# Layer 2's edge scores: the two channel halves' edge products set apart, their score products put together, ten edge buffers

## The chip, the cores and the metric

The kernel runs on one core of one Trainium2 chip. The metric is device time in microseconds (us) of one execution, as the median of several runs. A core has five engines that work side by side: TensorE (PE, matrix products; PEld is its weight load), VectorE (DVE), ScalarE (ACT), GpSimd (POOL) and SyncE (SP, which here only issues transfers). Each takes its own list of instructions in order, and semaphores make one engine wait for another.

## The reference

Four graph layers run one after another, each wrapped as `x = layernorm(x + layer(x, adj))`. The tensor x is 128 graphs x 64 nodes x 256 channels, all in f32. Only layer 2 is touched by the change:

```
Xq = (H @ W_lin.T).reshape(bt, n, 4, 64)          # 4 heads of 64 channels
Xv = (H @ W_val.T).reshape(bt, n, 4, 64)
e  = einsum('behd,hd->beh', leaky_relu(Xq[:, src] + Xq[:, dst], 0.2), a)   # 512 edges
e  = e + log(adj[src, dst] + 1e-8)
attn = softmax of e over the edges that share a src
Y  = segment_sum(attn * Xv[:, dst], src);  return Y @ W_out.T
```

For every graph and each of its 512 edges the rows of Xq at the edge's two ends are added, passed through a leaky relu, and multiplied with a vector per head: these sums are the scores.

## The kernel before, in words

X, the running tensor, stays on the chip as 64 tiles of 128 rows (two graphs of 64 nodes) x 256 channels. The scores of layer 2 are made by the generator `scores()`, in 32 steps k of two tiles each, that is four graphs (b = 0, 1 within a tile, i = 0, 1 for the tile). A step consists of the following.

- `transposed(k)`: four full transposes of X on PE (L1988) into a PSUM tile m; DVE copies it to xT (L1990).
- `maps(k)`: eight PE instructions of 128 x 128 x 512 (L2000; an f32 product is two instructions in the profile) make Xq and Xv in two PSUM tiles m; ACT copies them out as xq (L2004) and xv (L2014), and SP stores xv to DRAM (L2015) for later. The pool of m tiles has two buffers.
- For each channel half c = 0, 1 the edge products (L2037): four f32 products `xq.T @ GG` (GG holds a one at both ends of each edge), one for each (b, i), in the order (0,0), (1,0), (0,1), (1,1). Each uses 64 of the array's 128 rows: b = 0 the upper half, b = 1 the lower half. They write two PSUM tiles l (one for each i, with room for b = 0 and 1).
- ACT copies every l half to an edge buffer xs of 128 x 512 (L2044), and DVE applies the leaky relu in place (L2045). There are six xs buffers.
- `products()`: the score products (L1976), four f32 products of 128 rows x 32 columns, which add xs times the head vectors to the PSUM tile sc of this half c. They are called one half late: the products of the half before are issued behind the edge products of this half.

Beside this, the generator `last_pass()` finishes layer 1, four steps of it for each k: ACT scales Y (L1893), PE transposes it into an m tile (L1902), DVE adds it to X and gathers statistics (L1234, L1237, L1238), and once in each k a `Norm.flush()` takes a square root on ACT (L1214), five small DVE instructions (L1215 to L1249) and four normalisations of 128 x 256 on ACT (L1253). It lasts until k = 14. From k = 15 on the softmax of the first half of the graphs (`softmax(0)`, from L2059) is woven in, and from k = 26 on `values()`: products of 64 x 64 (L2143) and the output product (L2164).

The source order is a priority and not the order of execution: the framework's scheduler fixes the order of each engine's instructions when the program is built, and may place a later instruction ahead of one whose inputs are not due yet. `after(ins, those)` adds dependencies by hand: before the change the first of a half's four edge products waits for all earlier copies out of l and m (`taken`), so that the four stand together, and the first score product is ordered behind the last edge product and waits for all leaky relus of its half.

Of the kernel before, what the change touches and what calls it, by code (L numbers as in the profile page):

```python
# [7 lines left out]
F32 = mybir.dt.float32  # L8
I32 = mybir.dt.int32
AF = mybir.ActivationFunctionType  # L10
ALU = mybir.AluOpType
# [3 lines left out]
N = 64  # L15
NB = 128
D = 256
P = 128
E = 512
# [1240 lines left out]
def tile_adj_resnorm(ctx: ExitStack, tc: tile.TileContext, I: dict, out: bass.AP, layers: int = 4):  # L1260
    nc = tc.nc
    v, s, te = nc.vector, nc.scalar, nc.tensor
# [10 lines left out]
    for b in range(2):  # L1273
        r, o = slice(b * N, (b + 1) * N), slice((1 - b) * N, (2 - b) * N)
# [235 lines left out]
    with tc.tile_pool(name="lw", bufs=1) as lw, tc.tile_pool(  # L1510
        name="l0c", bufs=1
    ) as lc, tc.tile_pool(name="l0p", bufs=2, space=PSUM) as pp, tc.tile_pool(
        name="l0r", bufs=1, space=PSUM
# [196 lines left out]
        with tc.tile_pool(name="l0g", bufs=1) as l0:  # L1710
            back = iter(())
            for g in range(NT // TG):
# [7 lines left out]
                last, more = H, iter(())  # L1720
# [203 lines left out]
    HU = HT // 2  # L1924
    with ExitStack() as l2:
# [4 lines left out]
        sx = own1(scoring, name="l2x", bufs=2, side="right")  # L1930
        pg = own1(scoring, name="l2g", bufs=2, space=PSUM)
        pc = own1(scoring, name="l2c", bufs=2, space=PSUM)
        edge_s = lt.tile([P, WE], F32, tag="edge_s", name="edge_s")
        nc.sync.dma_start(edge_s, edge_d)
        GG, OS, lg, br, OE, ix = edge_tables(edge_s)
# [10 lines left out]
        az = lt.tile([P, 2, 3 * HU - 1], F32, tag="az", name="az")  # L1946
# [3 lines left out]
                o = (h + 1) * HU - 1  # L1950
                v.tensor_tensor(az[:, c, o : o + 1], heads[:, h : h + 1], acol[:, c : c + 1], ALU.mult)
        bf, bb = br[:, :E], br[:, 1:]
        sc, M2 = [None, None], [None, None]

        xvd = [dl.tile([P, 2, D], F32, tag=f"xv{k}", name=f"xv{k}") for k in range(NT // 2)]

        taken, late = [], []
        beside = [iter(())]
        soft = []

        def after(ins, those, how=mybir.DependencyClass.Sync):
            for i in those:
                tc.add_manual_dep(ins.ins, i.ins.name, mybir.DependencyInfo(how, mybir.DependencyReason.DATA),
                                  reason="together")

        def products():

            k, c, xs, ready = late.pop()
            half, u_ = divmod(k, HU)
            if u_ == 0 and c == 0:  # L1970
                sc[half] = [pc.tile([P, 512], F32, tag="sc", name="sc") for _ in range(2)]
            mms = []
            for b in range(2):
                for i in range(2):
                    q = 32 * (2 * b + i)
                    mms.append(te.matmul(sc[half][c][q : q + 32, :], az[:, c, HU - 1 - u_ : 3 * HU - 1 - u_],  # L1976
                                         xs[b, i], start=(u_ == 0), stop=(u_ == HU - 1)))
            after(mms[0], ready)
            if u_ == HU - 1:
                run(*[soft[half]] * (2 if half and not c else 1))  # L1980
            return mms[0]

        def transposed(k):

            ps = pp.tile([P, 512], F32, tag="m", name="m")
            for i in range(2):
                for c in range(2):
                    te.transpose(ps[:, i * D + c * P : i * D + (c + 1) * P], X[:, 2 * k + i, c * P : (c + 1) * P], ident)  # L1988
            xT = sx.tile([P, 2, 2, P], F32, tag="xT", name="xT", bufs=1)
            v.tensor_copy(xT.rearrange("p i c n -> p (i c n)"), ps)  # L1990
            return xT

        def maps(k, xT, apart=False):

            xq, xv = [], sx.tile([P, 2, D], F32, tag="xv", name="xv")
            pss = [pp.tile([P, 512], F32, tag="m", name="m") for _ in range(2)]

            def product(i, cols):
                for c in range(2):
                    te.matmul(pss[i][:, cols], xT[:, i, c, :], wqv[:, c, cols], start=(c == 0), stop=(c == 1))  # L2000

            def first(i):
                xq.append(sx.tile([P, D], F32, tag="xq", name="xq", bufs=4))
                taken.append(s.copy(xq[i], pss[i][:, :D]))  # L2004

            if apart:
                for i in range(2):
                    product(i, slice(0, D))
                    first(i)
            for i in range(2):  # L2010
                product(i, slice(D, 2 * D) if apart else slice(0, 2 * D))
                if not apart:
                    first(i)
                s.copy(xv[:, i, :], pss[i][:, D:])  # L2014
            nc.sync.dma_start(xvd[k], xv)  # L2015
            return xq

        def scores():


            K = NT // 2
            xT = transposed(0)
            xq = maps(0, xT, True)
            next(beside[0])
            next(beside[0])
            xT = transposed(1)


            four = [(b, i) for i in range(2) for b in range(2)]
            for k in range(K):  # L2030
                xn = None
                for c in range(2):
                    xs, pl = {}, [pg.tile([P, 2, 512], F32, tag="l", name="l") for _ in range(2)]
                    mms = []
                    for b, i in four:
                        r = slice(b * N, (b + 1) * N)
                        mms.append(te.matmul(pl[i][:, b, :], xq[i][r, c * P : (c + 1) * P], GG[r, :], start=True, stop=True))  # L2037
                    after(mms[0], taken)
                    del taken[:]
                    next(beside[0], None)  # L2040
                    ready = []
                    for b, i in four:
                        x = xs[b, i] = sx.tile([P, E], F32, tag="xs", name="xs", bufs=6)
                        taken.append(s.copy(x, pl[i][:, b, :]))  # L2044
                        ready.append(v.scalar_tensor_tensor(x, x, 0.2, x, ALU.mult, ALU.max))  # L2045
                    if late:
                        after(products(), mms[-1:], mybir.DependencyClass.NoSync)
                    late.append((k, c, xs, ready))
                    if c == 0 and k < K - 1:
                        xn = maps(k + 1, xT)  # L2050
                    if c == 1 and k < K - 2:
                        xT = transposed(k + 2)
                    next(beside[0], None)
                xq = xn
                if k == K - 1:
                    products()
                yield

        def softmax(half):  # L2059
# [108 lines left out]
        def run(*steps):  # L2168
            for x in steps:
                next(x, None)  # L2170

        bank = None
        scratch = lambda: bank() if bank else pp.tile([P, 512], F32, tag="m", name="m")
        sc_, beside[0] = scores(), last_pass()
        run(*beside * 4)
        run(*[sc_] * (NQ - 1))
# [40 lines left out]
        with tc.tile_pool(name="l3s", bufs=2) as s3, tc.tile_pool(name="l3p", bufs=6, space=PSUM) as p3:  # L2217
# [3 lines left out]
            four = lambda a: a.rearrange("p (j n) -> p j n", j=4)  # L2221
# [121 lines left out]
```

## Time and profile before

| | us |
|---|---|
| median of three runs | 2368.93 (2366.29 to 2371.05) |
| the profiled execution | 2368.87 |
| its span on the core | 2367.1 |
| edge products (L2037) first and last start | 1786.2 and 2156.9 |
| PE busy in the span | 2282.1 (96%) |
| DVE busy | 1804.4 (76%) |
| ACT busy | 971.7 (41%) |
| PE busy on L2037, 512 instructions | 134.0 |
| PE busy on L1976, 512 instructions | 68.2 |
| ACT busy on L2044, 256 instructions of 585 ns | 136.6 |
| DVE busy on L2045, 256 instructions of 683 ns | 165.9 |

Every stretch of time is read from the start of the span. In the timeline a row stands for a run of like instructions: start, length from the first start to the last end, engine, line, operation, output <- inputs, shape, count, and in brackets the idle time of the engine before it with what ended it. As PE instructions overlap at their ends, the step from one row's start to the next row's start is what a group takes.

### The profile page before, as it was taken

The page shows a single profiled execution, that of the slowest core. Times are in us where ns is not written, and L with a number is a line of the kernel's source. Part 1 is how long each engine was busy: PE and PEld are TensorE (multiplying, and loading weights), DVE is VectorE, ACT ScalarE, POOL GpSimd, SP SyncE. Part 2 cuts the span into 40 slices and gives each one's busy share as a digit, 9 for nine tenths or more (in the row PEclk, how much of TensorE's full clock was granted, in tenths as well). Part 3 has the DMA queues.
Part 4 walks back from the last instruction along what each step waited for, and adds up shares of the span by engine and source line. Part 5 has one row for each costly group of instructions (what it writes and reads, how often), then busy time and mean ns, then how long its engine had stood idle before and what let it go on. Part 6 is the DMA issues. An engine that isn't in the chain of part 4 may idle for free. (4 is left out here: it accounts for less than half of the span.)

```text
span 2367.1 us, 29693 instructions
## 1 busy us (share of the span) xinstructions
PE 2282.1 (96%) x9094; PEld 1228.0 (52%) x9094; DVE 1804.4 (76%) x8366; ACT 971.7 (41%) x1754; POOL 88.0 (4%) x134
## 2 busy tenths in 40 slices
PE   8999999999999999999999999999999999999897
PEld 6445654444665544664544544454434333445787
DVE  5666666677987888888889897787867886646587
ACT  2432232242333243332243322343437875557575
POOL 0000000000000000000000000000000000101431
PEclk9999999999999999999999999999999999999999
DMA  6000010100100010100101010011210010311532
GB/s 222 23 16 36 1 36 1 36 19 18 54 1 36 1 54 19 54 25 12 36 18 44 28 36 1 1 70 74 86 55 23 27 40 27 103 36 43 138 93 72
DMA packets 44662, 101.52 MB, mean 43 GB/s; under 512 B 5297, under 2 KB 23857, under 8 KB 43217
## 3 DMA queue, kind: packets, MB, share of 16 engines
q1 hardware_dynamic: 38656, 84.90, 10.6%
q0 software_dynamic: 3984, 14.40, 2.2%
q8 instruction: 72, 1.18, 0.2%
q14 instruction: 94, 0.76, 0.1%
q10 hardware_dynamic: 1856, 0.28, 0.1%
HBM read 67.97 MB, written 31.59 MB: 42 GB/s over the span
## 5 line engine op out<-in xcount | busy, mean ns | idle before, releaser
L1621 PE MATMUL pq<-H,wi 128*128 128x512 f32 (+1 forms) x2016 | 828.3, 547 | 4.6 <-DVE H L1671 4.0
L1648 ACT ACTIVATE gate<-pq,bl 128x512 f32<-128x512 f32 (+1 forms) x504 | 316.5, 633 | 761.6 <-PE pq L1626 618.7
L1621 PEld LDWEIGHTS pq<-H,wi 128*128 128x128 f32 x2016 | 372.3, 190 | 332.6 <-issue 255.8
L1626 PE MATMUL pq<-lh,wh 128*128 128x512 f32 (+1 forms) x1152 | 471.3, 533 | 12.0 <-DVE lh L1666 11.1
L1626 PEld LDWEIGHTS pq<-lh,wh 128*128 128x128 f32 x1152 | 215.1, 190 | 210.9 <-issue 135.0
L2045 DVE SCALAR_TENSOR_TENSOR xs<-xs 128x512 f32<-128x512 f32 x256 | 165.9, 683 | 57.0 <-ACT xs L2044 56.0
L2044 ACT COPY xs<-l 128x512 f32<-128x512 f32 x256 | 136.6, 585 | 73.8 <-PE l L2037 40.5
L1664 ACT ACTIVATE gate<-lc 128x512 f32<-128x512 f32 (+1 forms) x144 | 83.6, 580 | 183.0 <-DVE lc L1660 85.3
L2037 PE MATMUL l<-edge_s,xq 64*128 64x512 f32 x512 | 134.0, 616 | 9.5 <-ACT xs L2044 4.8
L2000 PE MATMUL m<-wqv,xT 128*128 128x512 f32 (+1 forms) x264 | 121.0, 595 | 0.9 <-DVE xT L1990 0.8
L1811 PE MATMUL ps<-at,w 128*128 128x512 f32 x256 | 116.7, 607 | 4.0 <-ACT at L1807 3.5
L1861 PE MATMUL ps<-h,w 128*128 128x512 f32 x256 | 112.3, 596 | 2.4 <-ACT h L1855 2.4
L1253 ACT ACTIVATE X<-X,ln_sh,ln_rs 128x256 f32<-128x256 f32 x192 | 99.9, 591 | 31.1 <-DVE ln_sh L1249 22.9
L142 DVE COPY AQR<-eps 64x192 f32<-64x192 f32 (+1 forms) x125 | 35.1, 281 | 94.3 <-PE eps L148 94.3
L1237 DVE BATCH_NORM_STATS2 ln_st<-X 128x6 f32<-128x256 f32 x256 | 98.6, 416 | 2.4
L2000 PEld LDWEIGHTS m<-wqv,xT 128*128 128x128 f32 x264 | 46.7, 189 | 73.9 <-issue 55.0
L1861 PEld LDWEIGHTS ps<-h,w 128*128 128x128 f32 x256 | 47.9, 190 | 60.7 <-issue 50.7
L1811 PEld LDWEIGHTS ps<-at,w 128*128 128x128 f32 x256 | 47.1, 192 | 59.9 <-issue 46.9
L2037 PEld LDWEIGHTS l<-edge_s,xq 64*128 64x128 f32 x512 | 46.1, 186 | 60.6 <-issue 31.7
L1671 DVE TENSOR_TENSOR H<-gate 128x512 f32<-128x512 f32 (+1 forms) x72 | 46.7, 649 | 30.5 <-ACT gate L1664 27.0
L129 DVE SCALAR_TENSOR_TENSOR CS<-GA,qE 64x1 f32<-64x1 f32 x294 | 61.7, 210 | 9.6
L1976 PE MATMUL sc<-xs,az 128*32 128x512 f32 x512 | 68.2, 605 | 0.6 <-DVE xs L2045 0.5
(585 smaller groups left out, 3200.5 us busy)
## 6 DMA issues: line engine op xcount, KB each, us to landing
wi<-in_WihT_dram SPq DMA_DIRECT2D x16, 1024.0 KB, 4.9
wh<-in_WhhT_dram SPq DMA_DIRECT2D x12, 1024.0 KB, 6.7
xd<-X SPq DMA_DIRECT2D x16, 512.0 KB, 3.0
X<-xd SPq DMA_DIRECT2D x16, 512.0 KB, 3.4
xv<-xv SPq DMA_DIRECT2D x32, 256.0 KB, 2.0
xr<-xv POOLq DMA_DIRECT2D x32, 256.0 KB, 3.0
X<-in_x_dram SPq DMA_DIRECT2D x15, 512.0 KB, 8.9
out_dram<-X SPq DMA_DIRECT2D x15, 512.0 KB, 2.9
```

What stands on the lines that cost most here:

```text
L1237: nc.vector.bn_stats(st, self.X[:, k, :])
L1253: nc.scalar.activation(x, x, AF.Identity, bias=sh[:, k : k + 1], scale=rs[:, k : k + 1])
L1621: te.matmul(ps, wi[:, kk, o * P : (o + 1) * P], at(kk, k), start=(kk == 0), stop=(k == 0 and kk == 1))
L1626: te.matmul(ahead[gt, c], wh[:, kk, o * P : (o + 1) * P], hst[:, kk, :M], start=False, stop=(kk == 1))
L1648: s.activation(gates[gt][:, c, :M], ps, AF.Tanh if gt == 2 else AF.Sigmoid, bias=bl[:, p - 1, o : o + 1])
L1664: s.activation(g[2], cs, AF.Tanh)
L1811: te.matmul(ps, w1[:, k, c * P : (c + 1) * P], at[:, k, :], start=(k == 0), stop=(k == 1))
L1861: te.matmul(ys[c], w2[:, k, c * P : (c + 1) * P], h[:, k, :], start=(k == 2), stop=(k == 1))
L2000: te.matmul(pss[i][:, cols], xT[:, i, c, :], wqv[:, c, cols], start=(c == 0), stop=(c == 1))
L2037: mms.append(te.matmul(pl[i][:, b, :], xq[i][r, c * P : (c + 1) * P], GG[r, :], start=True, stop=True))
L2044: taken.append(s.copy(x, pl[i][:, b, :]))
L2045: ready.append(v.scalar_tensor_tensor(x, x, 0.2, x, ALU.mult, ALU.max))
```

## The change

In step k the edge products of half 0 come first, then `last_pass` (two steps), the maps of step k + 1, `last_pass` again (two steps), the transposes for step k + 2, the edge products of half 1, and then, in one call, the score products of half 1 of step k - 1 and of half 0 of step k: eight in a row. The last step adds the products of its half 1. The edge buffers go from six to ten. The waits are by tile: the first product into the l tile of i waits for the copies out of the l tile of the same i one half earlier (`taken[i]`), and in half 0 for the copy of xq[i] (`mapped[i]`); the four edge products of a half no longer wait together. The first of the eight score products waits for the leaky relus of both its halves and is ordered behind the last edge product. The sc tiles are allocated one by one.

```diff
-        sc, M2 = [None, None], [None, None]
+        sc, M2 = [[None, None], [None, None]], [None, None]
...
-        taken, late = [], []
+        taken, mapped = {}, {}
...
-        def products():
-            k, c, xs, ready = late.pop()
...
+        def products(todo, held, last):
+            xss = [held.pop(x) for x in todo]
             mms = []
+            for (k, c), (xs, _) in zip(todo, xss):
+                half, u_ = divmod(k, HU)
+                if u_ == 0:
+                    sc[half][c] = pc.tile([P, 512], F32, tag="sc", name="sc")
+                for b in range(2):
+                    for i in range(2):
+                        q = 32 * (2 * b + i)
+                        mms.append(te.matmul(sc[half][c][q : q + 32, :], az[:, c, HU - 1 - u_ : 3 * HU - 1 - u_],
+                                             xs[b, i], start=(u_ == 0), stop=(u_ == HU - 1)))
+                if u_ == HU - 1:
+                    run(*[soft[half]] * (2 if half and not c else 1))
+            after(mms[0], [x for _, ready in xss for x in ready])
+            after(mms[0], [last], mybir.DependencyClass.NoSync)
...
-                taken.append(s.copy(xq[i], pss[i][:, :D]))
+                mapped[i] = s.copy(xq[i], pss[i][:, :D])
...
+            held = {}
+            def edges(c):
+                xs, ready = {}, []
+                for i in range(2):
+                    pl = pg.tile([P, 2, 512], F32, tag="l", name="l")
+                    for b in range(2):
+                        r = slice(b * N, (b + 1) * N)
+                        mm = te.matmul(pl[:, b, :], xq[i][r, c * P : (c + 1) * P], GG[r, :], start=True, stop=True)
+                        if not b:
+                            after(mm, taken.pop(i, []) + ([mapped[i]] if c == 0 else []))
+                    for b in range(2):
+                        x = xs[b, i] = sx.tile([P, E], F32, tag="xs", name="xs", bufs=10)
+                        taken.setdefault(i, []).append(s.copy(x, pl[:, b, :]))
+                        ready.append(v.scalar_tensor_tensor(x, x, 0.2, x, ALU.mult, ALU.max))
+                held[k, c] = xs, ready
+                return mm
             for k in range(K):
-                xn = None
-                for c in range(2):
...
+                edges(0)
+                xn = None
+                run(*beside * 2)
+                if k < K - 1:
+                    xn = maps(k + 1, xT)
+                run(*beside * 2)
+                if k < K - 2:
+                    xT = transposed(k + 2)
+                last = edges(1)
                 xq = xn
+                todo = [(k - 1, 1)] * (k > 0) + [(k, 0)]
+                products(todo, held, last)
                 if k == K - 1:
-                    products()
+                    products([(k, 1)], held, last)
                 yield
```

More of the change, by code (lines that the diff above doesn't have):

```diff
@@ L1964, in after @@
                                   reason="together")
-        def products():
-            k, c, xs, ready = late.pop()
-            half, u_ = divmod(k, HU)
-            if u_ == 0 and c == 0:
-                sc[half] = [pc.tile([P, 512], F32, tag="sc", name="sc") for _ in range(2)]
-            mms = []
[L1973 to L1981, printed above, removed]
+        def products(todo, held, last):
+            xss = [held.pop(x) for x in todo]
+            mms = []
+            for (k, c), (xs, _) in zip(todo, xss):
[11 more added lines that the diff above has]
+            after(mms[0], [last], mybir.DependencyClass.NoSync)
         def transposed(k):
@@ L2026, in scores @@
             xT = transposed(1)
-            four = [(b, i) for i in range(2) for b in range(2)]
+            held = {}
[14 more added lines that the diff above has]
+                return mm
@@ L2030, in scores @@
             for k in range(K):
+                edges(0)
                 xn = None
-                for c in range(2):
[L2033 to L2053, printed above, removed]
```

## The prediction

> **What bounds the kernel now.** I read the page's busy shares, then the windows, then the timeline of one score step, since all that changes lies between 1786 and 2162 us.
>
> ```profile
> PE 2282.1 (96%) x9094; PEld 1228.0 (52%) x9094; DVE 1804.4 (76%) x8366; ACT 971.7 (41%) x1754; POOL 88.0 (4%) x134
> ```
> ```profile
> 1900.00:1950.00 50.00, 48.82 (x230) 19.52 (x229) 42.93 (x113) 39.23 (x87) 0.00 (x0) 1.00 0.12 37
> ...
> 2000.00:2050.00 50.00, 49.78 (x238) 20.54 (x237) 29.88 (x47) 26.26 (x57) 8.94 (x9) 1.00 0.11 35
> ```
> PE, the first number after the length, is full in both stages. Beside the last pass DVE has 42.93 of 50 and ACT 39.23; later both have room. One step beside the last pass (PE and two rows of ACT):
> ```profile
> 1862.67 1.99 PE L2037 MATMUL l<-edge_s,xq 64*128 64x512 f32 x8
> ...
> 1864.59 1.07 PE L1976 MATMUL sc<-xs,az 128*32 128x512 f32 x8
> ...
> 1865.59 0.66 PE L1988 MATMUL m<-ident,X 128*128 128x128 f32 x4
> ...
> 1866.08 0.60 PE L1902 MATMUL m<-ident,y 128*128 128x128 f32 x4
> ...
> 1866.71 2.08 ACT L1253 ACTIVATE X<-X,ln_sh,ln_rs 128x256 f32<-128x256 f32 x4
> 1866.80 0.30 PEld L2037 LDWEIGHTS l<-edge_s,xq 64*128 64x128 f32 x4 [0.36 <-ACT xs L2044]
> 1866.80 1.99 PE L2037 MATMUL l<-edge_s,xq 64*128 64x512 f32 x8
> ...
> 1868.69 1.04 ACT L2044 COPY xs<-l 128x512 f32<-128x512 f32 x2
> ...
> 1868.72 1.07 PE L1976 MATMUL sc<-xs,az 128*32 128x512 f32 x8
> ...
> 1869.71 3.70 PE L2000 MATMUL m<-wqv,xT 128*128 128x512 f32 x8
> ...
> 1873.25 0.60 PE L1902 MATMUL m<-ident,y 128*128 128x128 f32 x4
> ```
> The next step's edge products start at 1873.88: 11.20 us a step (half 0 from 1866.80, half 1 at 1873.88). From start to start: a half's edge products 1.92, its score products 0.99, maps 3.54, transposes then edge products 0.62. The edge rows work in pairs, one for each half of the rows: 8 instructions take four slots of 0.43. ACT shows one more thing: the copy at 1868.69 could have started 1.18 after its products (2006.43 to 2007.61 elsewhere), at 1867.98, but stood behind four normalisations. PE had other work meanwhile.
>
> The price of a lone edge product is in the later stage:
> ```profile
> 2089.78 1.12 PE L2037 MATMUL l<-edge_s,xq 64*128 64x512 f32 x2 [0.24 <-ACT xs L2044]
> ...
> 2090.83 1.99 PE L2164 MATMUL m<-wo,yT 128*128 128x256 f32 x8
> ...
> 2092.76 1.98 PE L2037 MATMUL l<-edge_s,xq 64*128 64x512 f32 x6
> ...
> 2093.92 1.07 ACT L2044 COPY xs<-l 128x512 f32<-128x512 f32 x2 [2.68 <-PE l L2037]
> ...
> 2094.67 1.07 PE L1976 MATMUL sc<-xs,az 128*32 128x512 f32 x8
> ```
> One product alone takes 1.05, and the other three still 1.91, as much as all four. The copy of the first l tile waits for both its products, so it starts only 1.16 after the second.
>
> **The change part by part.** It removes and adds no arithmetic; it moves instructions. I read the new order from the built program, with what each instruction waits for. In steps 2 to 14 PE runs:
>
> ```
> edge 0 (i=0: 2 products), L1902 x3, edge 0 (i=1: 2), L1902 x1, maps 8,
> L1902 x4, edge 1 (1 product), L1988 x4, edge 1 (3 products), score products (16)
> ```
> The scheduler has split both halves, since the four no longer wait together. ACT runs: copy l1/i0, square root, copy l1/i0, four normalisations, two copies l1/i1, four copies of edge 0, then Y, xq, xv.
>
> *First stage, PE alone.* sc 1.91 (four slots 1.71 and a change to the row products, 0.2), edge pair 1.06, L1902 x3 0.51, pair 1.06, L1902 0.2, maps 3.54, L1902 0.62, lone 1.05, L1988 0.62, three 1.91: 12.48, so 1.28 above 11.20. The step from score products straight to edge products occurs nowhere in the trace; its bounds are 0 and 0.21 (edge to score, 1.92 less four slots); nearest is score to full, 0.14. I take 0.2. It costs nothing here, as the wait below covers it.
>
> *First stage, the new wait.* The second pair of edge 0 needs the l tile of i = 1, so it needs the two copies l1/i1, which ACT holds behind the normalisations. With t = 0 at L1988: three edge products from 0.62; first copy 0.62 + 1.18 = 1.80; the square root after it at 2.3 (its input, after L1990 at 0.63 to 1.31 and the statistics, is there at 1.7); leaky relu 2.41 (copy + 0.61), reciprocal 3.05, second relu 3.25 (0.64), four small DVE steps (1854.50 to 1855.31: 0.2 each) bring the shift at 4.50, normalisations at 4.69 (+0.19), the next copy 1.99 later (1855.50 to 1857.49) at 6.68, both done at 7.74, PE goes on at 7.80. PE alone would be there at 6.0: it waits 1.8. From there: pair 1.06, L1902 0.2, maps 3.54, L1902 0.62, lone 1.05, and L1988 again at about 14.24. The step grows by 3.04. Twelve of them (L1988 of step 1 to that of step 13): **+36.5**. Entry: L1988 of step 1 falls at about 1807.5 (1786.23 and the same rows, with about 1.4 of waits), so step 2 starts at 1811.9 against 1810.79: +1.1. Step 14 runs 12.6 against 13.07, and 0.6 of waits in the steps before goes: -1.0.
>
> *Ten edge buffers.* The two copies l1/i1 need buffers that the first score products free, at score start + 1.08 (2008.35 to 2009.43) = 3.6, before 6.68: nothing here. Later they run from 9.1 to 10.2 of a step and edge 0's second pair is due at 10.8: hidden by 0.6; without that cover it costs up to 0.5 a step.
>
> *Later stage, steps 15 to 25* (1958.84 to 2076.63, 117.8). Mostly the halves stay whole: edge 1.92, maps 3.54, L1988 0.62, edge 1.92, score 1.91: 9.91 against 10.19 (1996.24 to 2006.43), as four changes of tile shape stand where six were. Eleven times -0.28 is -3.1; step 16 has a lone product (+1.2); and before had already run four map instructions when step 15 began, 1.9, while after must still run them. Waits of 3.2 (softmax) I keep: about **0** (+0.5 taken).
>
> *Steps 26 to 30* (2076.63 to 2148.41, 71.8). Before, a lone edge product is split off in each; after, only in step 26, and L2143 and L2164 stand behind the score products. A step: 9.91 + 0.90 (L2143) + 1.92 (L2164) less 0.06 = 12.7, and about 0.35 in which L2164 waits for ACT's copy yT. Three such, step 26 with two L2143 groups 15.1, step 30 without L1988 12.4: 66.6, **-5.2**.
>
> *Step 31* (2148.41 to 2161.83, 13.4). Both edge halves stand together; the second waits for copies until 2.3 and 3.4 after the start, score products at 4.4, the last four at 7.5, end at 8.5: -4.9. But one L2164 and six L2143, 2.2, move behind the end: **-2.7**. The transfers keep their number and their place behind their copies: SP's xv stores follow the xv copies as before, POOL's loads follow L2143.
>
> *Sum* on the profiled execution, 2368.87 (median of the runs 2368.93, no difference): +1.1 + 36.5 - 1.0 + 0.5 - 5.2 - 2.7 = +29.2, 2398.1 us.
>
> The Trainium skill, TensorEngine Tiling (Array Packing), section Key Properties, says that a change of tiling mode drains the array; TensorE: Matmul & The Clock Gate, Step-by-step, gives a drain of about 128 cycles. The rows above show more, 0.14 to 0.21 a change. By an estimate from that page (128 cycles at 2.4 GHz, 0.05) the -3.1 of steps 15 to 25 would be about -1.2, and the sum 2400.
>
> **The rivals.**
>
> *B: the copies come in time.* If the second pair's wait doesn't show, the step is PE's own 12.48: 12 x 1.76 and as much in step 14 less, 22.9: 2375. For it: in the row at 1868.69 the same copies stood behind the same block at no cost. Against: there the next edge pair was 5 us away.
>
> *C: the later stage gives nothing back*, because copies, yT and the normalisations of `values` queue on one ACT as in 2139.55 to 2144.28, where PE already waited. Without the -5.2 and -2.7: 2406.
>
> *D, the other side: faster.* The first stage is held by DVE and not by PE's order: 42.93 of 50 is 9.6 us in 11.20, and DVE's work is unchanged. If the step stays at 11.20 whatever PE's order, the +36.6 falls away: 2361.5. It decides where a step grows by less than 7.4 / 12 = 0.6, below 11.8 us. Against it: PE has 48.82 of 50, and the lone product alone adds 1.05.
>
> **How the numbers follow.** My sum 0.64, B 0.14, C 0.17, D 0.05. A measurement tells about 0.2%, 4.7 us, from no change. The range 2377 to 2409 holds my own case (2388 to 2406 by itself: a step of 13.6 to 14.6) and C with three more for longer waits; it leaves out D and most of B. B at 2375 is itself just beyond the bound for slower, so a part of it counts as the same: slower 0.91, same 0.04, faster 0.05.
>
> **What would show it.** Right: L2037 in rows of x2 and x6 (after: its new line) in steps 2 to 14, one step about 14.2, PE's second pair with an idle time near 1.8 put down to ACT's copies, L1253 x4 right before them; plain later steps of 9.9; no edge split beside L2143 after step 26. Wrong: steps near 12.5 (B), later steps still near 14 (C), steps near 11.2 (D). What would spoil the sum is a different wait in the first stage, such as maps on L1234 (I have 0.1 of room there), or score to edge costing far from 0.2.

## The result, and the profile after

The changed kernel takes 2382.54 us (median of 5 runs, 2381.23 to 2393.78) against 2371.05 us for the kernel before on the same chip (2366.29 to 2373.65). The ratio is 1.0063 with a 95% interval of 1.0041 to 1.0086: slower, as forecast, at about half of the forecast amount; 2382.5 lies in the range of 2377 to 2409, but below the 2388 that the forecast gave its own case alone. The means differ by 14.9 us, the medians by 11.5. The profiled execution took 2386.70 us (span 2384.9), above the median of its five, and 17.8 us more than the one of before; its sum is compared below.

In the changed kernel the edge products are L2038, the score products L1977, the maps L2001, the transposes of X L1989, ACT's copies L2043 and DVE's leaky relus L2044. The busy line of the page, and then two of the windows (length; PE, PEld, DVE, ACT, POOL busy; clock, DMA share, GB/s):

```profile
PE 2288.8 (96%) x9094; PEld 1231.8 (52%) x9094; DVE 1804.3 (76%) x8366; ACT 968.1 (41%) x1752; POOL 88.4 (4%) x134
```
```profile
1900.00:1950.00 50.00, 45.34 (x199) 17.44 (x197) 34.64 (x94) 32.86 (x76) 1.66 (x3) 1.00 0.11 38
2000.00:2050.00 50.00, 48.34 (x210) 18.87 (x210) 34.16 (x51) 28.56 (x62) 0.00 (x0) 1.00 0.06 22
```

The whole kernel's shares say nothing: 96% for PE in both. The window beside the last pass does: PE fell from 48.82 to 45.34 of 50 and carries out 199 instructions where it had done 230. One step of that stage in the timeline (start, length, engine, line; in brackets the idle time before it and what ended it):

```profile
1861.76 0.66 PE L1989 MATMUL m<-ident,X 128*128 128x128 f32 x4
...
1862.35 1.98 PE L2038 MATMUL l<-edge_s,xq 64*128 64x512 f32 x6
...
1863.50 0.59 ACT L2043 COPY xs<-l 128x512 f32<-128x512 f32 x1 [1.49 <-PE l L2038]
1863.99 0.21 ACT L1214 ACTIVATE is_s<-is_t 128x4 f32<-128x4 f32 x1
1864.09 0.58 ACT L2043 COPY xs<-l 128x512 f32<-128x512 f32 x1
...
1864.26 1.92 PE L1977 MATMUL sc<-xs,az 128*32 128x512 f32 x16
...
1866.11 1.13 PE L2038 MATMUL l<-edge_s,xq 64*128 64x512 f32 x4
1866.19 2.07 ACT L1253 ACTIVATE X<-X,ln_sh,ln_rs 128x256 f32<-128x256 f32 x4 [1.52 <-DVE ln_sh L1249]
...
1867.17 0.55 PE L1902 MATMUL m<-ident,y 128*128 128x128 f32 x3
1868.17 2.01 ACT L2043 COPY xs<-l 128x512 f32<-128x512 f32 x4
...
1869.27 1.13 PE L2038 MATMUL l<-edge_s,xq 64*128 64x512 f32 x4 [1.55 <-ACT xs L2043]
1870.33 0.33 PE L1902 MATMUL m<-ident,y 128*128 128x128 f32 x1
...
1870.50 3.60 PE L2001 MATMUL m<-wqv,xT 128*128 128x512 f32 x8
...
1873.93 0.60 PE L1902 MATMUL m<-ident,y 128*128 128x128 f32 x4
...
1874.46 1.12 PE L2038 MATMUL l<-edge_s,xq 64*128 64x512 f32 x2
...
1875.52 0.66 PE L1989 MATMUL m<-ident,X 128*128 128x128 f32 x4
```

From one L1989 to the next a step takes 13.76 us; it took 11.20. Edge 0 is in two pairs, half 1 has its lone product (1.06 from 1874.46 to 1875.52), and the second pair of edge 0 stops PE for 1.55. The reason stands in ACT's rows: the copies of the second l tile come at 1868.17, behind four normalisations at 1866.19, and those had themselves let ACT idle for 1.52 until DVE had their shift. The products that these copies read were done by 1864.3. The Trainium skill, TensorE: Matmul & The Clock Gate, in its opening table, calls the queue of ScalarE strictly first in, first out; these rows agree, 3.9 us of it. Summed over the stage (1800 to 1970), the waits of PE (in all, times, longest; before, from 1800 to 1960, PE waited 2.7 us in all and never for these copies):

```profile
PE l L2038 <- ACT xs L2043: 18.6, 12, 1.6
PE m L2001 <- DVE X L1234: 0.9, 1, 0.9
```

In the later stage PE has a step of 9.76 (1989.97 to 1999.73) where it had 10.19, and a value step of 12.89 (13.2 to 14.2 and more before), as no product stands alone in it:

```profile
2117.87 0.97 PE L2149 MATMUL m<-mc,xr 64*64 64x64 f32 x32
2119.02 1.99 PE L2170 MATMUL m<-wo,yT 128*128 128x256 f32 x8 [0.18 <-ACT yT L2152]
2120.95 1.99 PE L2038 MATMUL l<-edge_s,xq 64*128 64x512 f32 x8
2122.86 3.70 PE L2001 MATMUL m<-wqv,xT 128*128 128x512 f32 x8
2126.40 0.60 PE L1989 MATMUL m<-ident,X 128*128 128x128 f32 x4
2126.93 1.99 PE L2038 MATMUL l<-edge_s,xq 64*128 64x512 f32 x8
2128.85 1.92 PE L1977 MATMUL sc<-xs,az 128*32 128x512 f32 x16
```

### The profile page after: what moved, and what is told of

It reads as the page before. It is cut to its first block, busy times and chain, and to the rows that moved or that the text cites. A ratio compares the mean times of both kernels' runs of the same rounds, so it can differ in the third digit from the quotient of the medians.

```text
span 2384.9 us, 29702 instructions
## 1 busy us (share of the span) xinstructions
PE 2288.8 (96%) x9094; PEld 1231.8 (52%) x9094; DVE 1804.3 (76%) x8366; ACT 968.1 (41%) x1752; POOL 88.4 (4%) x134
## 5 line engine op out<-in xcount | busy, mean ns | idle before, releaser
L2044 DVE SCALAR_TENSOR_TENSOR xs<-xs 128x512 f32<-128x512 f32 x256 | 164.0, 685 | 81.3 <-ACT xs L2043 80.0
L2038 PE MATMUL l<-edge_s,xq 64*128 64x512 f32 x512 | 148.8, 624 | 20.5 <-ACT xs L2043 20.5
L2043 ACT COPY xs<-l 128x512 f32<-128x512 f32 x256 | 135.2, 590 | 73.1 <-PE l L2038 60.8
L2001 PE MATMUL m<-wqv,xT 128*128 128x512 f32 (+1 forms) x264 | 119.4, 594 | 1.8 <-DVE X L1234 0.9
L2038 PEld LDWEIGHTS l<-edge_s,xq 64*128 64x128 f32 x512 | 47.6, 185 | 78.3 <-issue 43.1
L2001 PEld LDWEIGHTS m<-wqv,xT 128*128 128x128 f32 x264 | 48.6, 195 | 61.3 <-issue 36.7
L129 DVE SCALAR_TENSOR_TENSOR GA<-qtg,CS,GA 64x1 f32<-64x1 f32 x294 | 61.8, 210 | 9.1
```

The costliest lines, as they stand in the source:

```text
L129: self.nc.vector.scalar_tensor_tensor(o, a, s, b, op0, op1)
L2038: mm = te.matmul(pl[:, b, :], xq[i][r, c * P : (c + 1) * P], GG[r, :], start=True, stop=True)
L2043: taken.setdefault(i, []).append(s.copy(x, pl[:, b, :]))
```

## The experiments

**How they are compared.** Profiled executions reach the transposes for step 1 at times between 1782.8 and 1793.3 us, although none of the kernels differs before the scores; the two latest had a mean granted clock of 0.988, the others 0.990 to 0.992. So the stages are counted from there: *first* is from the transposes for step 1 to those for step 16 (the expectations call these the second and the sixteenth), *rest* from there to the end of the span. *Step* is a plain step beside the last pass. The executions of the changed kernel, e3 and f3 have stretches of half clock inside these stages that the others lack; they are named where they matter. The ratio is to the kernel before, over all runs, with its 95% interval.

| kernel | step | first | rest | sum | ratio |
|---|---|---|---|---|---|
| before | 11.20 | 166.6 | 414.9 | 581.5 | 1 |
| changed | 13.75 | 200.0 | 399.2 | 599.2 | 1.0063 (1.0041 to 1.0086) |
| e1 late normalisations | 12.52 | 182.1 | 399.4 | 581.5 | 1.0003 (0.9993 to 1.0013) |
| e2 whole half 1 | 12.33 | 181.6 | 396.8 | 578.4 | 0.9993 (0.998 to 1.0007) |
| e3 eight buffers | 12.61 | 183.1 | 408.9 | 592.0 | 1.0057 (1.004 to 1.0073) |
| e4 old first stage | 11.30 | 168.4 | 396.7 | 565.1 | 0.9937 (0.992 to 0.9953) |
| f1 short normalisations | 13.23 | 190.6 | 398.9 | 589.5 | 1.0034 (1.0017 to 1.005) |
| f2 before, ten buffers | 12.06 | 176.8 | 409.1 | 586.0 | 1.0036 (1.0022 to 1.0051) |
| f3 before, paired scores | 11.01 | 165.1 | 413.1 | 578.2 | 0.9976 (0.996 to 0.9992) |
| f4 e1 and e2 together | 11.48 | 170.6 | 397.0 | 567.6 | 0.9954 (0.994 to 0.9968) |
| g1 f4, short normalisations | 10.74 | 161.3 | 397.0 | 558.3 | one run |
| g2 paired, then changed | 11.64 | 173.9 | 395.5 | 569.4 | 0.9942 (0.9921 to 0.9964) |
| g3 paired, then whole | 11.64 | 173.9 | 394.7 | 568.6 | 0.9952 (0.9932 to 0.9972) |
| h1 f4, normalisations on POOL | 10.74 | 160.7 | 397.5 | 558.2 | 0.9893 (0.9876 to 0.9909) |

**e1: the normalisations later.**

```diff
-                run(*beside * 2)
+                run(*beside)
                 if k < K - 2:
                     xT = transposed(k + 2)
                 last = edges(1)
+                run(*beside)
```

> One step of last_pass (the one that issues the flush with its four normalisations L1253) is called behind the edge products of half 1 instead of ahead of them; nothing else is edited. In the built order ACT now takes all four copies of half 1 ahead of the normalisations, and PE's edge 0 is whole again (8 instructions in a row), while half 1 keeps its lone product. Theory S (the prediction's: the step is PE's own rows plus the wait for copies that stand behind the normalisations): no wait at edge 0, and the step is the sum of the rows of the changed kernel: score 1.85, edge 0 1.92, L1902 0.57, maps 3.43, L1902 0.53, lone 1.05, transposes 0.58, three edge products 1.91 = 11.84 us instead of 13.75; some 12.5 steps of that are -24 us on the changed kernel's 2382.5: about 2359 (2356 to 2364). Rival R1 (the copies are late in any case, by DVE or by ACT's whole load, so that another wait of the same size appears): the step stays at 13.3 or more and the time at 2377 or more. Rival R2 (the stage is held by DVE, which needs 9.6 us of each step and the leaky relus in it): the step ends between, near 12.6, 2368.

Measured: 2371.09 us, a step of 12.52. The stop at edge 0 is gone, and edge 0 is whole, but the step is not the 11.84 of the rows. PE now stops in the middle of the maps (timeline of e1):

```profile
1876.50 1.99 PE L2038 MATMUL l<-edge_s,xq 64*128 64x512 f32 x8
...
1876.73 2.08 ACT L1253 ACTIVATE X<-X,ln_sh,ln_rs 128x256 f32<-128x256 f32 x4
...
1878.71 2.01 ACT L2043 COPY xs<-l 128x512 f32<-128x512 f32 x4
...
1879.31 1.29 DVE L2044 SCALAR_TENSOR_TENSOR xs<-xs 128x512 f32<-128x512 f32 x2 [1.41 <-ACT xs L2043]
...
1880.52 0.68 DVE L1234 TENSOR_TENSOR X<-m,X 128x512 f32<-128x512 f32 x1
...
1881.25 1.99 PE L2001 MATMUL m<-wqv,xT 128*128 128x512 f32 x4 [0.46 <-DVE X L1234]
```

The same four normalisations now hold the copies of edge 0; DVE takes the leaky relus of two of those copies ahead of the X add, and the X add frees the m tile for the second four maps. The eight maps are four and four, 2.34 from start to start (1878.91 to 1881.25) instead of 1.71. So theory S had the right stop and missed the next one in line; R1 and R2 gave sizes near 13.3 and 12.6 for it, and whether it is DVE's load, as R2 says, or ACT's block was not yet decided. f1 and g1 were made for that.

**e2: half 1 whole.**

```diff
-                if k < K - 2:
-                    xT = transposed(k + 2)
                 last = edges(1)
+                if k < K - 2:
+                    xT = transposed(k + 2, [last])   # first transpose ordered behind last
```

> The transposes for step k + 2 are issued behind the edge products of half 1 and ordered behind their last one; nothing else is edited. In the built order half 1 is whole (8 instructions), so the lone product is gone, while edge 0 is still in two pairs and ACT still has the normalisations ahead of the last copy of half 1. Theory S: a lone product costs 1.05 and that is what is saved, and the wait for ACT stays: copies from 1.18 after the start of half 1, shift at about 4.6, normalisations 4.8 to 6.8, the last copy done at 7.4, where PE alone would be at 6.0 (1.92 + 0.6 + 1.9 + 1.06 + 0.5): a wait of about 1.4, a step of about 12.65 instead of 13.75, -14 us in all: about 2369 (2366 to 2373). Rival R3 (the lone product only fills the wait for ACT, so without it the wait is 1.05 longer): the step stays at 13.6 or more, 2380 or more. Rival R4 (the whole loss hangs on the lone product): the step falls back to 11.3, 2352.

Measured: 2367.77 us, a step of 12.33, with ACT's wait still there (1.13 idle before the second pair, put down to the copies). S gave 12.65 and 2369; R3 and R4 are out. The clean price of a lone product is had by comparing e1 with f4, which differ in this edit alone and have the same stop in the maps: 12.52 less 11.48 is 1.04.

**e3: eight buffers.**

```diff
-                        x = xs[b, i] = sx.tile([P, E], F32, tag="xs", name="xs", bufs=10)
+                        x = xs[b, i] = sx.tile([P, E], F32, tag="xs", name="xs", bufs=8)
```

> The edge buffers go from ten to eight in the changed kernel, one number. The built order changes with it: in steps 2 to 14 PE runs score 16, L1902 x4, two map instructions, edge 0 (8), six map instructions, L1902 x4, lone product, transposes, three edge products, and ACT takes the square root and the four normalisations ahead of all four copies of half 1. Theory S, from ACT's chain: transposes at 0, square root near 1.6, shift near 2.7, normalisations 2.9 to 4.9, four copies to 7.0, edge 0 at 7.05, where PE alone would be at 5.9; PE's own rows are 12.05, so the step is about 13.2 and the time about 2376 (2370 to 2382). If the number of buffers did nothing but hold back copies (rival R5: order apart, a buffer too few costs a wait at ACT), it would be slower than with ten: 2385 or more. If only PE's rows counted: 12.05 a step, 2361.

Measured: 2381.26 us, a step of 12.61. The first stage is 17 us shorter than with ten buffers, but the rest is 9.7 longer. The step came out 0.6 below S, because the first pair of edge 0 needs only the first two copies and not all four: edge 0 starts 1.10 after the first of them (1875.29 to 1876.39). The rest was not in any theory: in the value steps a product stands alone again ahead of L2170, 13.63 a step instead of 12.89. The stretch behind the scores is 5.8 longer (210.2 against 204.5): PE waits 3.28 there for yT, and in this execution the granted clock was 0.50 from 2180 to 2186, where the changed kernel had full clock at this point, so not all of the 9.7 is the order's. Beside the last pass the number of buffers acts through the order that the scheduler makes and not by holding copies back (R5): with eight as with ten, no copy of ACT waits there for score products to free a buffer (ACT's waits, 1800 to 1940).

**e4: the old first stage, the new rest.** For k < 15 the loop of before (with ten buffers), from 15 on that of the change:

```diff
-            for k in range(K):
+            for k in range(15):
+                for c in range(2):
...
+                    if held:
+                        products(list(held), held, mms[-1])
+                    held[k, c] = xs, ready
...
+            for k in range(15, K):
                 edges(0)
```

> Steps 0 to 14 are those of the kernel before (its order, its waits for all copies, its place of last_pass, score products one half late); from step 15 on the loop is that of the changed kernel; ten buffers throughout. Theory S (the loss is all in steps 2 to 14, and the later stage gives back some 12 us by itself): first stage as before, l0 of step 15 near 1958.8, plain later steps of 9.76, steps 26 to 30 of 12.89, score products end near 2149: about 2358 against 2371 before, 0.5% faster (2354 to 2363). Rival C (the later gain is only the remains of the first stage's delay, work that was put off or softmax work that had become ready in the longer time): waits of the softmax come back in steps 16 to 25, and the time is 2366 to 2372.

Measured: 2353.97 us, at the lower end of S's range. The rest takes 396.7 us by itself, 18 less than before where S had said some 12, and the first stage 168.4 against 166.6: the loss was in the first stage, as S has it, and the later gain doesn't need it. Rival C of the prediction (nothing comes back later) is out. The first stage is not quite the old one: 11.30 a step, with L1902 ahead of the score products in the order built with ten buffers.

**f1: the block of normalisations cut short** in the changed kernel; of the tiles normalised in this stage only one column is, so this part of the computation is left out.

```diff
+                x = x[:, :1] if n == 4 and self.n == 8 else x
                 nc.scalar.activation(x, x, AF.Identity, bias=sh[:, k : k + 1], scale=rs[:, k : k + 1])
```

> The changed kernel with the four normalisations of each flush of last_pass cut to one column of each tile (the other 255 columns of those tiles are left as they are, so that part of the computation is left out); ACT's order in a step stays that of the changed kernel (copy, square root, copy, four normalisations, copies), only the block gets shorter, from 2.0 to some 0.8 us. Theory S (the length of ACT's block is the wait, and the copies behind it also hold DVE's leaky relus and with them the X add that the maps wait for): no wait of PE at edge 0 and none in the maps, the step at the rows' own 11.84, 13.75 less 1.91, and about -24 us in the first stage: 2359. In the run with later normalisations the step came to 12.52, with 0.46 to 0.63 of waiting in the maps on DVE's X; here that should be gone too. Rival R6 (the 12.5 of the runs with late normalisations, a whole half 1 or eight buffers, 12.52, 12.33 and 12.61, are a limit of DVE or of the two m tiles and not of the block): 12.3 or more again, 2368 or more.

Measured: 2377.66 us, a step of 13.23. The order on ACT stayed (timeline of f1, where lines are one higher):

```profile
1878.90 1.22 ACT L1254 ACTIVATE X<-X,ln_sh,ln_rs 128x1 f32<-128x1 f32 x4 [1.53 <-DVE ln_sh L1249]
1880.03 2.01 ACT L2044 COPY xs<-l 128x512 f32<-128x512 f32 x4
...
1881.13 1.13 PE L2039 MATMUL l<-edge_s,xq 64*128 64x512 f32 x4 [1.18 <-ACT xs L2044]
```

The block holds the copies 1.13 (1878.90 to 1880.03) instead of 1.98 (1866.19 to 1868.17), 0.85 less. The second pair comes 6.66 after the transposes (1874.47) instead of 7.51 (1861.76 to 1869.27): also 0.85 less. So what ACT does ahead of the copies passes to PE one for one. It does not go to nothing, which was the error in the expectation: most of the delay is not the block but the wait ahead of it, 1.53 for DVE's shift, and the copies stand behind that too. The step fell by 0.52 only, because three L1902 that had filled the stop now stand behind it.

**f2 and f3: the parts alone, in the kernel before.** f2 changes one number; f3 also issues the score products of both halves together, with all waits as before.

```diff
-                        x = xs[b, i] = sx.tile([P, E], F32, tag="xs", name="xs", bufs=6)
+                        x = xs[b, i] = sx.tile([P, E], F32, tag="xs", name="xs", bufs=10)
```
```diff
-                    if late:
-                        after(products(), mms[-1:], mybir.DependencyClass.NoSync)
                     late.append((k, c, xs, ready))
+                    while c and len(late) > 1:        # products() takes late.pop(0)
+                        after(products(), mms[-1:], mybir.DependencyClass.NoSync)
```

> The kernel before with ten edge buffers instead of six, one number. In the built order the first stage runs edge 0, L1902, score 8, maps, L1902, edge 1, score 8, transposes (the same order as in the run with the old first stage, 11.30 a step), and in the value steps 27 to 30 the halves stay whole but for two steps, while score products still come in eights. Theory S (tile changes are counted in rows, lone products cost 1.05): plain later steps stay at 10.19 as the number of tile changes is the same; value steps fall from 14.18 to about 13.1 where no product is alone, 3 x 1.1; the first stage +0.1 a step, +1.3: about 2367 (2363 to 2371). Rival R7 (the buffers alone give the later gain): 2356 or less. Rival R8 (buffers alone do nothing, order unchanged in effect): 2369 with value steps of 14.2.

> The kernel before with ten edge buffers and the score products of both halves issued together behind the edge products of half 1; the waits for all copies, the place of last_pass and of the transposes stay those of before. In the built order steps 1 to 14 run edge 1 (8), score 16, transposes, edge 0 (8), L1902, maps, L1902: no product is alone. Theory S: rows 1.92 + 1.85 + 0.6 + 1.92 + 0.57 + 3.43 + 0.6 = 10.9, and a wait of 0 to 0.4 in the maps on DVE's X, since the normalisations end about 0.6 after the copies of edge 0 are due: a step of 10.9 to 11.3 instead of 11.20, nothing lost in the first stage; the later stage as in the changed kernel, -10 to -16: about 2355 (2350 to 2360). Rival R9 (pairing itself hurts beside the last pass, by leaky relus that come late for sixteen score products at once): a step of 12 or more, 2368 or more.

Measured: f2 2379.20 us, slower than before, with a step of 12.06 in which the maps stop for 0.63 on DVE's X; the later plain steps stay at 10.19, two of the value steps fall to 12.3 and 13.1. The expectation called f2's order the same as e4's and took 11.30 a step from there; but f2 has the second L1902 ahead of edge 1 and e4 behind it, and the maps stop in f2 and not in e4. f3 2364.51 us, a step of 11.01: pairing costs nothing beside the last pass (R9 is out), and its plain later steps take 10.05 or less. But its rest, 413.1, is hardly better than before's. New stops of 1.58 on the copy of xq and 1.64 on that of xv stand in two late steps, and others behind the scores. Beside that, this execution has three stretches of 3.41 us with a granted clock of 0.5 (from 2137.9, 2158.3 and 2168.6), with PE busy nearly throughout, that the one of before has not; by half of their length they cost some 5 us (an estimate). So ten buffers alone make the kernel slower, and the pairing with them gives at most a part of the later gain. Which part of the change's loop makes the rest of it, its order or its waits by tile, is not shown; f3 was not taken apart further.

**f4 and g1: both edits, and the block cut short again.** f4 is e1 and e2 together:

```diff
-                run(*beside * 2)
-                if k < K - 2:
-                    xT = transposed(k + 2)
+                run(*beside)
                 last = edges(1)
+                if k < K - 2:
+                    xT = transposed(k + 2, [last])
+                run(*beside)
```

g1 is f4 with f1's edit, and leaves out what f1 leaves out. The built orders of PE, ACT and DVE are the same in the two.

> The changed kernel with both edits of the first runs: one step of last_pass behind the edge products of half 1, and the transposes ordered behind those products. In the built order every half is whole in both stages. Theory S: the two savings do not add (1.23 and 1.42 a step from 13.75 would give 11.1), since the wait for DVE's X in the maps stays: rows 1.92 + 0.6 + 1.9 + 1.92 + 0.57 + 3.43 + 0.6 = 10.95, plus 0.2 to 0.6: a step of 11.2 to 11.6, #later steps 9.91 as with the whole half 1: about 2354 (2349 to 2361). Rival R6 (a limit near 12.3 beside the last pass whatever PE's order): 2367 or more.

> The kernel with late normalisations and a whole half 1 (11.48 us a step, with a stop of 0.47 to 0.64 in the maps put down to DVE's X), with the four normalisations cut to one column each, so that part of the computation is left out as in the run with short normalisations; the built order of PE, ACT and DVE is the same as without the cut. Theory S2 (the stop in the maps is a chain: normalisations on ACT, the copies of edge 0 behind them, the leaky relus of these copies on DVE, the X add behind the relus, the m tile that the maps need): the block is some 0.85 us shorter, the stop of 0.64 goes, the step is 10.85 to 10.95. Rival R10 (the X add is late by itself, by DVE's own load or by the transposed y): the step stays at 11.3 or more.

Measured: f4 2357.90 us, a step of 11.48, with the stop in the maps (timeline of f4):

```profile
1860.38 1.88 PE L2003 MATMUL m<-wqv,xT 128*128 128x512 f32 x4
1862.73 1.98 PE L2003 MATMUL m<-wqv,xT 128*128 128x512 f32 x4 [0.47 <-DVE X L1234]
```

g1: a step of 10.74 and the maps in one row (timeline of g1):

```profile
1873.46 0.66 PE L1903 MATMUL m<-ident,y 128*128 128x128 f32 x4
1873.95 3.60 PE L2004 MATMUL m<-wqv,xT 128*128 128x512 f32 x8
1877.39 0.60 PE L1903 MATMUL m<-ident,y 128*128 128x128 f32 x4
```

A shorter block on ACT, with DVE's work unchanged, removed a stop that was put down to DVE. That settles e1: the chain is normalisations, copies, leaky relus, X add, maps. R2, R6 and R10 (a limit of DVE) fall: DVE did the same work in 10.74 us a step.

**g2 and g3: paired first stage, changed rest.** The loop of e4 with the score products of a step together in steps 0 to 14; in g3 also e2's edit from step 15 on.

```diff
-                    if held:
+                    if c:
                         products(list(held), held, mms[-1])
```

> Steps 0 to 14 with the loop of the kernel before but the score products of both halves together behind the edge products of half 1 (and ten buffers), steps 15 to 31 with the loop of the changed kernel. Counted from the second transposes to the end of the span, the kernel before takes 581.5 us, of which 166.6 to the sixteenth transposes; the kernel with paired products took 165.1 for the first part, the one with the old first stage 396.7 for the second. Theory S (each stage's time is its own order's, so the parts add): 165 + 397 = 562, 19 less than before: about 2351 (2347 to 2356). In this built order L1902 stands ahead of the score products instead of ahead of edge 1; if that brings the stop in the maps back (0.6 a step), 2358.

> As the run before it in this set (paired products in steps 0 to 14), but from step 15 on the changed kernel's loop with the transposes ordered behind the edge products of half 1, so that no product of the later steps up to 25 is alone. Theory S: plain later steps 9.91 instead of 9.76, the steps with softmax without the 1.2 of a lone product; from the sixteenth transposes to the end 396.8 (as with the whole half 1 alone) instead of 396.7: no difference between the two, about 2351 (2347 to 2356).

Measured: 2355.75 and 2361.64 us. The stop in the maps came back (0.49 on DVE's X, a step of 11.64), the case that the expectation of g2 had named, at 2358. Neither beats e4. Between each other, rest 395.5 and 394.7, they don't differ.

**h1: the normalisations off ACT.** f4, with the block on an engine that is idle in this stage:

```diff
+            if self.act and n == 4 and self.n == 8:
+                nc.gpsimd.tensor_scalar(x, x, rs[:, k : k + 1], sh[:, k : k + 1], ALU.mult, ALU.add)
+                continue
```

> The kernel with late normalisations and a whole half 1, with the four normalisations of each flush beside the scores computed on POOL instead of ACT (tiles times the scale plus the shift, the same result); POOL has only 5.5 us of work before the score stage. Nothing is left out. Theory S2 (ACT's block holds the copies, and through them the relus, the X add and the maps): the block leaves ACT's queue, the step falls to the 10.74 measured with the block shortened, the first part to 161.3, and the whole from the second transposes to the end to 558, 23 less than before: about 2349, ratio 0.990 to 0.993. Rival R11 (POOL's four instructions, some 0.7 us each by the row of POOL's adds of 128x256, slow DVE's instructions while they run): the step stays at 11.2 or more, ratio 0.994 or more.

Measured: 2345.89 us (2343.80 to 2347.47), ratio 0.9893 (0.9876 to 0.9909): 1.1% faster than before, the best of all, with the whole computation in it. The timeline of h1:

```profile
1871.34 4.50 POOL L1253 TENSOR_SCALAR X<-X,ln_rs,ln_sh 128x256 f32<-128x256 f32 x4 [6.24 <-DVE ln_sh L1249]
...
1872.21 2.05 ACT L2048 COPY xs<-l 128x512 f32<-128x512 f32 x4 [0.87 <-PE l L2043]
1872.83 1.54 DVE L2049 SCALAR_TENSOR_TENSOR xs<-xs 128x512 f32<-128x512 f32 x2 [0.39 <-ACT xs L2048]
...
1873.44 3.60 PE L2006 MATMUL m<-wqv,xT 128*128 128x512 f32 x8
```

ACT takes the four copies of edge 0 as soon as their products are there (it waits for PE, 0.87), and the maps run through. (The two copies before them wait 1.22 for score products to free their buffers, and PE does not wait for that.) The block takes twice as long on POOL, 4.50 us against 2.08 on ACT, and nobody waits for it.

## Why the prediction was right, and where its numbers were off

The direction and its cause held: PE's split halves and ACT's block in steps 2 to 14, more than the later stage gives back. In the profiled executions, term by term, by the starts of edge 0:

| term | forecast | measured | from |
|---|---|---|---|
| entry, to step 2 | +1.1 | +0.3 | 1811.08 against 1810.79 |
| twelve steps | +36.5 | +30.7 | 12 x (13.76 - 11.20) |
| exit, step 14 | -1.0 | +0.1 | start of step 15 +31.1, less the two above |
| steps 15 to 25 | +0.5 | -1.9 | 115.9 against 117.8 |
| steps 26 to 30 | -5.2 | -5.6 | 66.2 against 71.8 |
| step 31 | -4.9 | -5.0 | 8.4 against 13.4 |
| work moved behind the scores | +2.2 | -0.8 | 204.4 against 205.2 |
| sum | +29.2 | +17.8 | |

- *The order* was as read: x2 and x6 rows, L1902 in three and one, the normalisations ahead of the copies. *The new wait* is where it was put, 1.55 where 1.8 was forecast.
- *The step* is the term that was mis-sized, 14.24 against 13.76; twelve times that is half of the error. (The forecast's own terms add up to 14.27.) The second pair came 7.51 after the transposes and not 7.80, since DVE's short chain to the shift, in the order that the working had, was quicker: the shift started at 4.24 and not 4.50. The first leaky relu started at 2.36 (2.41), the second one only 0.09 behind the reciprocal (0.20), and the small steps came 0.58 behind that (0.64).
- *PE from that pair on* took 6.25, where the forecast's terms add up to 6.47. The maps took 3.43 for 3.54: the 3.54 was read where maps follow score products and the first of them takes 0.53 instead of 0.43, and here they follow L1902, of the same shape. L1902 x4 took 0.53 for 0.62: the 0.62 held a wait of 0.09. In the kernel before, the edge products of half 1 waited for all earlier copies, and their weight load at 1873.88 is put down to ACT's copy of xq; by the change's waits by tile half 1 no longer waits for it. The single L1902 took 0.17 for 0.2.
- *Exit*: step 14 was forecast shorter, but its maps took 5.30 us instead of 3.60, and it is no shorter. The order is not the reason. In this execution the granted clock was 0.51 from 1980.50 to 1984.00, and four map instructions took 0.85 each instead of 0.43, 1.7 in all; without that the term is -1.6. The execution of before has no such stretch between 1800 and 2162; what set it off is not shown, nor whether the other executions have it.
- *Steps 15 to 25* were taken at 9.91 and came at 9.76, since the score products with the step to the edge products take 1.85 and not 1.91, and the transposes with that step 0.53 and not 0.62 (the wait for xq once more). It is a gain of 0.43 a step: 0.09 is that wait, and 0.34 goes with four changes of tile shape instead of six. The prediction's estimate, which took the drain of about 128 cycles in the Trainium skill, TensorE: Matmul & The Clock Gate, Step-by-step, as the price of a change, would have made these steps 10.1; the 9.76 speaks against that use of it.
- *Work moved behind the scores* costs nothing. This term failed in its cover: before, PE waited 0.65, 1.20 and 0.16 there for the softmax and yT, and in the changed kernel it waits for none of these, though it has 12 more L2149 and 8 more L2170 to do. The working had counted the moved instructions as if PE were full where they went. It is not full further on either: in both kernels PE then stands still for the load of xr, 7.70 before and 8.19 after, and the end of the scores lies 61.3 and 61.2 ahead of the end of that wait. The remaining 0.7 lies in the L2164 (L2170) row right behind it, 5.99 against 5.29, in which the granted clock rose from 0.5 to full.
- *The price of a lone product*, 1.05 from two rows of the later stage, held: 1.04 (e1 against f4).
- *Rivals.* B (no wait, 12.48 a step): the trace shows the wait twelve times, 18.6 us; in f1 its end moves with ACT's block one for one. C: e4 keeps the whole later gain without the first stage's loss. D, held by DVE: g1 and h1 run the stage at 10.74 with DVE's work unchanged. That the changed kernel's PE rows, less the wait, come to 12.21 shows what B had right: 1.0 of the 2.56 is PE's order, the lone product, and 1.55 is the wait.
- *Ten buffers* were costed at nothing as buffers, and that held beside the last pass: no copy waits there for score products. But the number of buffers changes the order, which the prediction took as built: 12.61 a step with eight, 13.76 with ten, and in the kernel before ten make it 0.36% slower.

## What to carry to other kernels

Read an in-order engine's queue for what stands behind an instruction that has to wait: here copies that were ready stood 3.9 us behind four normalisations whose input was late. Cutting the block short in its place gained only 0.52 a step, as the copies still stood behind the late input (f1); with the block behind the copies, cutting it short or moving it to an idle engine took the same 0.74 off the step (g1 and h1 against f4). When such a block is moved within the same queue, look at once for the next thing it will hold (from edge 0 to the X add and the maps, which took back 0.7 of the 1.9 us a step that the move should have gained). A change of loop order that helps one stage can be made for that stage alone: the same loop lost 33 us up to the transposes for step 16 (1.7 of it by the clock) and won 16 behind them.

## What the runs showed of the hardware that was not expected

- POOL and DVE slow each other by the kind of DVE instruction. Beside POOL's normalisations (h1, 1800 to 1930) single leaky relus of 128x512, two inputs on the chip, took up to 964 ns against 693 at most in f4, and POOL's own instructions of 128x256 from 545 to 2019 ns, 545 and 546 for the two that no leaky relu overlapped; X adds with one input in PSUM stayed at 0.68 to 0.69. The Trainium skill, SBUF — State Buffer, section Who interferes with whom, says that a DVE instruction with two SBUF inputs contends with a GpSimd instruction that reads SBUF; the rows agree. It cost the step nothing: 10.74 with it in h1 and without it in g1.
- The change from score products (128*32) to edge products (64*128) costs about what the other way does from score to full, 0.14: sixteen instructions take 1.85 with it, and four slots of 0.43 are 1.71. The prediction had 0 to 0.21 and took 0.2. (It says that this step occurs nowhere in the trace of before; it does once, at 2076.63, but behind a wait of 1.14, so that it gives no price.)
